# Layer 1's 3x3 convolutions by 4x4 output tiles and two images per pass, in place of 4x2 tiles and one image

## The chip, the cores and the metric

One core of a Trainium2 chip runs the whole program in one launch. The metric is the device time of one execution in microseconds; lower is better. In this text PE is TensorE (matmul), PEld its weight load, DVE is VectorE, ACT is ScalarE, POOL is GpSimd and SP is SyncE, which here only issues DMAs.

## The reference

The input x has 4 images of 512 channels, 32x32, in float32. Layer 0 is a Mamba block over the 1024 pixels of each image as tokens, layer 1 a position-attention block. Both are added to their input, and both take the input through a group norm. Layer 1 is what the change rewrites:

```python
x_top = conv1x1(x, w_top); x_center = conv1x1(x, w_center)     # 64 channels each
x_bottom = conv3x3(x, w_bottom)                                # 512 -> 512
sp = softmax over all pairs of pixels (x_center^T x_top)       # 1024 x 1024 per image
sp = sp @ x_bottom^T ; reshape to (512, 32, 32)
return conv3x3(x + sp, w_out)                                  # 512 -> 512
```

So each image needs two 3x3 convolutions with 512 channels in and out, called b (w_bottom) and o (w_out) below, with the attention between them.

## The kernel before

**Layer 0** is ordered by a planner of the kernel's own (`Plan`). Every step names its engine, an estimate of its time, what it reads and writes, and a due time (`prio`); a greedy pass over all steps writes each engine's queue in the order in which it would start them. The selective scan is cut into 32 blocks (4 images x 4 groups of 256 channels x 2 halves of 512 tokens) of 16 states each, one state of one block being one unit of due time, so that layer 0 runs from 0 to 512 in due times. Per unit, ACT makes the decay (L837) and the scaled input (L849), PE transposes (L875), DVE scans (L889), POOL or DVE multiplies by C (L911, L905) or POOL by B (L864), and PE adds up (L918). The projections of the next image and the output of the one before are spread between.

Also in layer 0, as filler steps (`fill=True`) with due times of their own, lie the weight pieces: the convolutions are Winograd convolutions, and their transformed weights are made on the chip. `transform(u, src, k, prio)` makes piece k of 16 for one convolution: 128 input channels by 128 output channels. POOL does all its additions (three over 768 elements, L1185 to L1195, and nine over 256, L1203 to L1205), ACT two scalings (L1177, L1178), and SP stores the result to the DRAM tensors `u_b` and `u_o` (L1212). The pieces use scratch cut from a tile called `work`, which later becomes the first image's tile. They come at

```python
for k in range(2 * NPC):                       # NPC = 16 pieces per convolution
    transform(u, src, k % NPC, -5 if k < PRM['t0'] else PRM['tg'] * (k - PRM['t0']))
```

with t0 = 7 and tg = 18.5: seven before the first unit, the others one per 18.5 units. `first_image` loads and normalises image 0 at the end of layer 0.

**Layer 1** has no planner: it is written in program order, and the framework (Tile) lists each engine's queue, earlier instructions first when they can run. For each image b the code is: `scores(b)` (1x1 convolutions, the 1024x1024 product `psc`, exponentials `st`), `conv3("b{b}")`, `attend` (product `pat` of `st` with the convolution's result, added into the image xg), `conv3("o{b}")`, transposition back and output. `norm(b + 1)` is drawn through a generator between the first products of `attend`.

A convolution works on tiles of 4x2 outputs: 8 x 16 = 128 tiles per image, one per PE row. The input transform first combines rows (tiles `e`, `f`, `g`, `h`, `k`, `l`, `rr`), in three pairs (1,2), (3,4), (0,5) of the six row indices p, on ACT, POOL and DVE, then columns into `v` (four column indices q, L1488 to L1491, DVE). For each of the 6 x 4 = 24 pairs (p, q) PE accumulates four chunks of 128 channels into a PSUM bank `m` (five banks), with the weights `uw` loaded from u (L1499, L1503); a bias product (L1508) is added at (1,1). ACT and DVE take m into `n` (L1511, L1519), POOL and DVE combine the rows into `y` (L1524 to L1543). For `o`, PE transposes `y` back (`po`, L1589) and DVE adds it to the layer's input (L1594), which is stored to the output.

Of the kernel before, what the change touches and what calls it, by code (L numbers as in the profile page):

```python
# [8 lines left out]
F32 = mybir.dt.float32  # L9
AF = mybir.ActivationFunctionType  # L10
# [161 lines left out]
def mamba_then_pab_kernel(  # L172
# [54 lines left out]
    for name, src in (("b", b_bottom), ("o", b_out)):  # L227
        t = cpool.tile([1, C], F32, tag=f"brow_{name}", name=f"brow_{name}")
        nc.scalar.dma_start(
            t.rearrange("o (c p) -> o c p", p=P), src.rearrange("p (c o) -> o c p", o=1)  # L230
        )
        nc.scalar.activation(t, t, AF.Copy, scale=-12.0)
        brow.append(t)

    def padded(b, pool, tag):

        xg = pool.tile([P, NCC, HH + 2, WW + 2], F32, tag=tag, name=f"xg_{b}")
        nc.gpsimd.memset(xg[:, :, 0, :], 0.0)
        nc.gpsimd.memset(xg[:, :, HH + 1, :], 0.0)
        nc.gpsimd.memset(xg[:, :, 1 : HH + 1, 0], 0.0)  # L240
        nc.gpsimd.memset(xg[:, :, 1 : HH + 1, WW + 1], 0.0)
        return xg

    NP6, NQ = 6, 4
    ub, uo = (
        [
            dram.tile([NP6, P, NCC, C], F32, tag=f"u_{n}_{q}", name=f"u_{n}_{q}")
            for q in range(NQ)  # L250
        ]
        for n in "bo"
    )
    x1 = [
# [25 lines left out]
    with ExitStack() as l0:  # L280
# [53 lines left out]
        work = cpool.tile([P, NCC * (HH + 2) * (WW + 2)], F32, tag="image", name="work")  # L334
# [6 lines left out]
        def dram_set(name, shape, n=B):  # L341
# [10 lines left out]
            "tg": 1, "tm": 1, "tp": 1, "tn": 1, "to": 2,  # L352
# [38 lines left out]
        for ring, rows in (("tg", 9), ("tm", 6), ("tp", 6), ("tn", 6), ("to", 4), ("to", 4)):  # L391
            cells.setdefault(ring, []).append(work[:, at * QC : (at + rows) * QC])
            at += rows
# [689 lines left out]
        def first_image(prio):  # L1083

            spl = {}
            stat = buf(None, None, "")
            chunks = [buf(None, None, "") for c in range(NCC)]

            def inner(c):
                return image[0][:, c, 1 : HH + 1, 1 : WW + 1]  # L1090

            def make():
                image[0] = padded(0, cpool, "image")

            step("POOL", 1.2, make, [], [pieces, *chunks], prio - PRM["fl"])
            for c in range(NCC):
                for h in range(NH):
                    n = HH // NH
                    step(
                        "SP", 0.4,  # L1100
                        lambda c=c, h=h, n=n: nc.sync.dma_start(
                            inner(c)[:, h * n : (h + 1) * n, :],
                            x1[0][h][c * P : (c + 1) * P, :].rearrange("p (h w) -> p h w", w=WW),
                        ),
                        [x1s[0][h]], [chunks[c]], prio - PRM["fl"], kb=768,
                    )

                def stats(c=c):
                    if c == 0:
                        spl["mv"] = spool.tile([P, NCC, 2], F32, tag="mv", name="mv_image")  # L1110
                    bs = spool.tile([P, NH, 6], F32, tag="bs", name=f"bs_image_{c}")
                    n = HH // NH
                    for h in range(NH):
                        nc.vector.bn_stats(bs[:, h, :], inner(c)[:, h * n : (h + 1) * n, :])
                    nc.vector.bn_aggr(spl["mv"][:, c, :], bs)

                step("DVE", 1.45, stats, [chunks[c]], [stat], prio + 4)
            prio += 4
            pm = buf("mm", [P, T], "pm_image")
# [571 lines left out]
```

## Time and profile before

| | |
|---|---|
| three timed runs | 3069.58, 3080.04, 3082.79 us (median 3080.04) |
| the profiled execution's own time | 3079.09 us |
| its span in the profile | 3077.3 us |
| granted TensorE clock, mean | 0.97 of full |
| busy share of the span: PE, DVE, ACT, POOL | 91%, 74%, 59%, 69% |
| layer 0 / layer 1 | 0 to 2044 us / 2044 to 3077 us |

A group of the profile is one line of the source on one engine with its operation, output and inputs: x its count, busy time in us, the mean of one in ns, then the idle time of the engine ahead of it and who ended that. A float32 matmul shows as two PE records. Where a helper issues the instruction, groups are told apart by the names of the tiles.

### The profile page before, as it was taken

What the parts mean: (1) busy time and instruction counts of PE and PEld (TensorE: products, weight loads), DVE (VectorE), ACT (ScalarE), POOL (GpSimd) and SP (SyncE); (2) the same over time, 40 slices, a digit from 0 to 9 for tenths busy, and PEclk for the clock granted to TensorE, in tenths of its full rate; (3) what the DMA queues carried; (4) which work ended last, traced back from release to release, by engine and by line L of the source; (5) the groups of instructions that cost most, each with busy time, mean ns of one, the idle gap of its engine ahead of it and who ended that gap; (6) DMA issues with size and microseconds to landing.
All of it is one profiled execution on the core that took longest, in us unless ns stands there. A gap on an engine that the chain in (4) does not pass through costs nothing.

```text
span 3077.3 us, 36921 instructions
## 1 busy us (share of the span) xinstructions
PE 2789.0 (91%) x11896; PEld 1669.4 (54%) x11896; DVE 2290.1 (74%) x2989; ACT 1822.0 (59%) x3300; POOL 2125.4 (69%) x1197
## 2 busy tenths in 40 slices
PE   6788789999889999888999968879999999999998
PEld 2556566566666666666666656644444444444444
DVE  4579999888999988989988879985285375346344
ACT  4679878898888888788898879941120030030000
POOL 6989888899978899978889999952151143134222
PEclk9899899999999999999999989999999999999999
DMA  6756455577645577745567654448178458628827
GB/s 183 219 171 210 142 158 155 174 233 241 210 139 173 179 222 239 237 128 162 164 189 222 213 159 140 134 121 319 43 266 316 155 175 317 245 85 312 302 86 260
DMA packets 404537, 600.07 MB, mean 195 GB/s; under 512 B 47192, under 2 KB 246104, under 8 KB 379768
## 3 DMA queue, kind: packets, MB, share of 16 engines
q1 hardware_dynamic: 395536, 583.18, 59.8%
q10 hardware_dynamic: 8648, 14.26, 1.3%
q8 instruction: 95, 1.56, 0.2%
q14 instruction: 98, 0.80, 0.1%
q0 software_dynamic: 160, 0.26, 0.0%
HBM read 500.60 MB, written 96.99 MB: 194 GB/s over the span
## 4 chain that ended last, share of the span: by engine, by line
PE 40%; DVE 12%; ACT 6%; DMA 4%; POOL 4%; issue 3%; SPq 0%; DVEq 0%; POOLq 0%; ACTq 0%
PE m_o L1503 10%; PE m_b L1503 8%; PE pat L1553 7%; DVE da L889 5%; PE y L918 3%; PE po L402 2%; PE psc L1380 2%; PE u L875 2%; DMA uw_b<-u_b 2%; POOL da L911 2%; DVE dbx L889 2%; DVE u L889 1%; PE pz L402 1%; PE pp L728 1%; ACT sc L849 1%
## 5 line engine op out<-in xcount | busy, mean ns | idle before, releaser
L911 POOL TENSOR_TENSOR da<-da,cbc 128x1024 f32<-128x1024 f32 x328 | 773.2, 2368 | 114.7 <-DVE da L889 53.1
L849 ACT ACTIVATE sc<-dtxt,bt_sb 128x256 f32<-128x256 f32 x1312 | 578.1, 499 | 99.3 <-PE u L875 98.5
L837 ACT ACTIVATE da<-dt,a_sb 128x512 f32<-128x512 f32 x656 | 454.1, 716 | 78.8 <-PE y L918 62.8
L864 POOL TENSOR_TENSOR dbx<-dtx,bbc 128x1024 f32<-128x1024 f32 x184 | 434.4, 2373 | 10.6 <-DVE carry_sb L894 4.6
L889 DVE TENSOR_TENSOR_SCAN da<-da,carry_sb,u 128x512 f32<-128x512 f32 x328 | 403.1, 1262 | 42.4 <-PE u L875 40.1
L918 PE MATMUL y<-ident,da 128*128 128x128 f32 x2624 | 366.6, 284 | 72.1 <-POOL da L911 69.9
L889 DVE TENSOR_TENSOR_SCAN da<-da,u 128x512 f32<-128x512 f32 x328 | 397.9, 1213 | 31.0 <-PE u L875 29.0
L875 PE MATMUL u<-ident,sc 128*128 128x128 f32 x2624 | 389.2, 282 | 23.5 <-DVE da L889 14.8
L918 PEld LDWEIGHTS y<-ident,da 128*128 128x128 f32 x2624 | 309.4, 146 | 180.6 <-POOL da L911 132.3
L875 PEld LDWEIGHTS u<-ident,sc 128*128 128x128 f32 x2624 | 314.2, 145 | 113.5 <-issue 34.2
L1503 PE MATMUL m_b<-uw_b,v_b 128*128 128x512 f32 x768 | 337.6, 596 | 17.5 <-issue 8.3
L1503 PE MATMUL m_o<-uw_o,v_o 128*128 128x512 f32 x768 | 334.1, 595 | 4.5 <-DVE v_o L1422 4.1
L402 PE MATMUL pxm<-xt,winc 128*128 128x341 f32 (+4 forms) x768 | 251.0, 470 | 21.7 <-DVE xs L661 10.5
L1503 PEld LDWEIGHTS m_b<-uw_b,v_b 128*128 128x128 f32 x768 | 143.4, 190 | 204.1 <-issue 187.1
L402 PE MATMUL pz<-xt,winc 128*128 128x512 f32 x512 | 244.8, 599 | 8.8 <-DMA winc<-in_w_in_dram 2.5
L837 ACT ACTIVATE u<-dt,a_sb 128x512 f32<-128x512 f32 x368 | 245.5, 681 | 11.9 <-DVE da L889 6.7
L1503 PEld LDWEIGHTS m_o<-uw_o,v_o 128*128 128x128 f32 x768 | 145.6, 191 | 190.2 <-issue 181.7
L918 PE MATMUL y<-ident,dbx 128*128 128x128 f32 x1472 | 215.4, 285 | 36.0 <-DVE dbx L905 24.7
L918 PEld LDWEIGHTS y<-ident,dbx 128*128 128x128 f32 x1472 | 175.7, 147 | 88.2 <-DVE dbx L905 25.8
L1553 PE MATMUL pat<-y_b,st 128*128 128x512 f32 x512 | 221.7, 593 | 0.1
L661 DVE SCALAR_TENSOR_TENSOR xs<-pxm,cw_sb,xs 128x341 f32<-128x341 f32 (+8 forms) x288 | 163.6, 569 | 60.6 <-ACT xs L652 53.6
L1511 ACT ACTIVATE e_b<-m_b 128x512 f32<-128x512 f32 x24 | 14.3, 596 | 316.4 <-PE m_b L1503 300.0
(220 smaller groups left out, 4315.4 us busy)
## 6 DMA issues: line engine op xcount, KB each, us to landing
cbc<-bcd SPq DMA_DIRECT2D x512, 256.0 KB, 3.6
uw_b<-u_b SPq DMA_DIRECT2D x96, 1024.0 KB, 5.1
uw_o<-u_o SPq DMA_DIRECT2D x96, 1024.0 KB, 4.9
bbc<-bcd SPq DMA_DIRECT2D x184, 256.0 KB, 3.9
u_b<-work SPq DMA_DIRECT2D x192, 128.0 KB, 3.0
u_o<-work SPq DMA_DIRECT2D x192, 128.0 KB, 3.4
winc<-in_w_in_dram SPq DMA_DIRECT2D x72, 256.0 KB, 3.7
szd<-sz SPq DMA_DIRECT2D x32, 512.0 KB, 4.0
```

The costliest lines, as they stand in the source:

```text
L402: lambda k=k, lhs=lhs, rhs=rhs: nc.tensor.matmul(p()[:, at : at + cols], lhs(), rhs(), start=(k == 0), stop=(k == n - 1)),
L661: nc.vector.scalar_tensor_tensor(u()[:, first:end], p()[:, first - k - at + before : n - k + before], cw[k], u()[:, first:end], ALU.mult, ...
L837: nc.scalar.activation(t, dt()[:, j], AF.Exp, scale=a_sb[:, at : at + 1])
L849: nc.scalar.activation(sc()[:, k], dtxt()[:, k], AF.Copy, scale=bt[:, at, s : s + 1])
L864: lambda: nc.gpsimd.tensor_mul(hc(), dtx(), b_bc().to_broadcast([P, 2, T])),
L875: nc.tensor.transpose(u()[:, k * P : (k + 1) * P], sc()[:, k, j, :], ident)
L889: nc.vector.tensor_tensor_scan(ht, *((hc()[:, j], u()) if on_act else (u(), hc()[:, j])), carry_sb[:, j, s : s + 1] if h else 0.0, ALU.mul ...
L911: lambda: nc.gpsimd.tensor_mul(hc(), hc(), c_bc().to_broadcast([P, 2, T])),
L918: nc.tensor.matmul(y[j]()[:, k, :], hc()[:, j, k * P : (k + 1) * P], ident, start=(s == 0 and k == 0), stop=(s == NS - 1 and k == NK - 1), ...
L1380: nc.tensor.matmul(pt, top[:, m * P : (m + 1) * P], center[:, h * T : (h + 1) * T], start=True, stop=True,)
L1503: nc.tensor.matmul(m[q], v[:, q, k, c, :], w[:, c, :], start=(c == 0), stop=(c == NCC - 1 and not extra),)
L1553: nc.tensor.matmul(pt, st[m][:, 2 * P * j + h : 2 * P * (j + 1) : 2], xb[m // 2][:, m % 2, :], start=(m == 0), stop=(m == NMC - 1),)
```

## The change

Layer 1 takes tiles of 4x4 outputs: 36 products per tile in place of 24, with 8 x 8 = 64 tiles per image, so that two images fill the 128 rows of one pass. The images lie in SBUF sorted by the remainder of row and column mod 4 (`grid`, pitch 9), with zeros where a border is needed. The loop goes over pairs of images. Rows and columns both use the six-point transform (`rows`, `cols`); intermediates `e`, `h`, `m0` of the columns lie in PSUM. The attention goes image by image; `by_image` sorts the first convolution's result by image with ACT copies. Behind the first image's attention the first row pair of the second convolution is made for that image, and for the second image chunk by chunk.

The weight pieces grow with it: in layer 0 a piece has two column steps per row group where it had one (POOL), two more scalings on ACT per row group, and 18 stores where it had 12. Only 16 + EARLY = 22 pieces are made there, at the due times that pieces 0 to 21 had. The other ten, all of w_out, are made by `piece` on DVE, written behind the attentions of the first pair of images. `first_images` also takes the statistics of image 1; `norm` of images 2 and 3 comes at the head of the second pair's turn.

```diff
-    NP6, NQ = 6, 4
+    NP = 6
+    PITCH = 9
+    SIDE = 4 * PITCH
+    FIRST = (26, 0, 9, 18, 27, 1)
+    def grid(xg, c):
+        return xg[:, c].rearrange("p (b y) (k x) -> p b y k x", y=PITCH, x=PITCH)
...
+    def normalise(xg, c, t, scale, bias):
+        v = t.rearrange("p (y b x k) -> p b y x k", y=8, b=4, x=8)
+        for b in range(4):
+            nc.scalar.activation(
+                grid(xg, c)[:, b, 0:8, :, 0:8].rearrange("p y k x -> p y x k"), v[:, b],
+                AF.Identity, bias=bias[:, c : c + 1], scale=scale[:, c : c + 1],
+            )
...
-                step(name, 2.28, columns, [b], [o], prio, fill=True)
-                for q in range(NQ):
...
+                step("ACT", 0.9, more, [b], [sc], prio, fill=True)
+                for q in (1, 3, 0):
+                    if q:
...
+                        step(name, 2.28, columns, [b, sc] if q == 3 else [b], [o], prio, fill=True)
+                    for k, qq in enumerate((q, q + 1) if q else (0, 5)):
...
-        for k in range(2 * NPC):
+        for k in range(NPC + EARLY):
...
+        def wide(name):
+            return lp.tile([P, L], F32, tag="a", name=name, bufs=16)
...
+        def rows(pair, r, m, cs=slice(0, NCC)):
+            xg = image[m]
+            x = [xg[:, cs, a : a + TI, :].rearrange("p c i x -> p c (i x)") for a in FIRST]
+            r0, r1 = (t[m][:, cs].rearrange("p c i x -> p c (i x)") for t in r)
+            if pair == (1, 2):
+                stt(r0, x[2], -4.0, x[4], ALU.mult, ALU.add)
+                stt(r1, x[1], -4.0, x[3], ALU.mult, ALU.add)
+                (nc.vector if cs.stop - cs.start == 1 else nc.gpsimd).tensor_sub(r1, r0, r1)
+                stt(r0, r0, 2.0, r1, ALU.mult, ALU.subtract)
+            elif pair == (3, 4):
+                nc.gpsimd.tensor_sub(r1, x[4], x[2])
+                nc.gpsimd.tensor_sub(r0, x[3], x[1])
+                stt(r1, r0, -2.0, r1, ALU.mult, ALU.add)
+                stt(r0, r0, 4.0, r1, ALU.mult, ALU.add)
+            else:
+                stt(r0, x[2], -5.0, x[4], ALU.mult, ALU.add)
+                stt(r0, x[0], 4.0, r0, ALU.mult, ALU.add)
+                stt(r1, x[3], -5.0, x[5], ALU.mult, ALU.add)
+                stt(r1, x[1], 4.0, r1, ALU.mult, ALU.add)
...
+        def cols(name, r, v, m=slice(0, 2), cs=slice(0, NCC)):
...
+            e, h, m0 = (bank(f"{t}_{name}")[:, :n] for t in ("e", "h", "m0"))
...
+            eng = nc.gpsimd if n == 2 * NCC * HT else nc.vector
+            stt(shaped(e), x[2], -4.0, x[4], ALU.mult, ALU.add)
+            stt(shaped(f), x[1], -4.0, x[3], ALU.mult, ALU.add)
+            tt.tensor_sub(w[2], laid(e), laid(f))
+            tt.tensor_add(w[1], laid(e), laid(f))
+            eng.tensor_sub(shaped(g), x[4], x[2])
+            tt.tensor_sub(shaped(h), x[3], x[1])
+            stt(w[4], laid(h), -2.0, laid(g), ALU.mult, ALU.add)
+            stt(w[3], laid(h), 2.0, laid(g), ALU.mult, ALU.add)
+            tt.tensor_sub(shaped(m0), x[2], x[0])
+            stt(w[0], laid(m0), -4.0, laid(g), ALU.mult, ALU.add)
+            eng.tensor_sub(shaped(m3), x[5], x[3])
+            stt(w[5], laid(h), -4.0, laid(m3), ALU.mult, ALU.add)
...
+                    for q in (2, 1, 4, 3, 0, 5):
...
+                        if q in (2, 4):
+                            nc.scalar.activation(e, m[q], AF.Copy, scale=w[q])
+                        elif q == 1 and not edge:
+                            stt(n[0][:, 0], m[1], w[1], e, ALU.mult, ALU.add)
+                            stt(n[0][:, 1], m[1], w[1], e, ALU.mult, ALU.subtract)
+                        elif q == 1:
...
+                        elif q == 3:
+                            stt(m[4], m[3], w[3], e, ALU.mult, ALU.subtract)
+                            stt(m[3], m[3], w[3], e, ALU.mult, ALU.add)
+                            src = n if edge else (n[0], n[0])
+                            stt(n[1][:, 0], m[3], 4.0, src[1][:, 0], ALU.mult, ALU.add)
+                            stt(n[1][:, 1], m[4], 8.0, src[1][:, 1], ALU.mult, ALU.add)
+                            tt.tensor_add(n[0][:, 0], m[3], n[0][:, 0])
+                            stt(n[0][:, 1], m[4], 2.0, n[0][:, 1], ALU.mult, ALU.add)
+                        else:
+                            t = n[q // 5][:, q // 5]
+                            stt(t, m[q], w[q], t, ALU.mult, ALU.add)
...
+        def piece(k):
...
+            for x in range(3):
+                t = lp.tile([P, 2 * NCC, QC], F32, tag="u", name=f"g_{k}_{x}", bufs=5)
+                nc.sync.dma_start(t[:, 0:6:5], taps[:, x, 0:3:2])
+                nc.sync.dma_start(t[:, 6], taps[:, x, 1])
+                tt.tensor_add(t[:, 1], t[:, 0], t[:, 5])
...
+            for q, far, near in ((1, 1.0, 1.0), (3, 4.0, 2.0)):
...
+                stt(f[0], g[2], far, g[0], ALU.mult, ALU.add)
+                stt(f[1], g[1], -near, f[0], ALU.mult, ALU.add)
+                stt(f[0], g[1], near, f[0], ALU.mult, ALU.add)
...
+        for b in range(0, B, 2):
+            if b:
+                norm(b)
+            norm(b + 1)
+            sa = scores(b)
+            conv3(f"b{b}", ub, brow[0], after=by_image(b, xb))
+            sb = scores(b + 1)
+            attend(b, *sa, xb)
+            r = row_tiles(name, (1, 2), True)
+            v = {p: v_tiles(f"{name}_{p}") for p in (1, 2)}
+            rows((1, 2), r, 0)
+            for k, p in enumerate((1, 2)):
+                cols(f"{name}_{p}_a", r[k], v[p], slice(0, 1))
...
+            attend(b + 1, *sb, xb, chunk)
+            if b == 0:
+                for k in range(EARLY, NCC * C // QC):
+                    piece(k)
+            conv3(name, uo, brow[1], v, back(b, b + 2 == B))
```

In the sums of rows (`conv3`, not shown) POOL makes the sums and differences of a row pair's `n` tiles (eight of 1024 elements in the pairs (1,2) and (3,4) together, and two more into y[0]), and DVE six scaled sums of 1024. `back` loads both images' layer input into eight tiles of the ring "a" ahead of the convolution, and stores them after the last row.

## The prediction

> **What bounds the kernel now.** I read the busy shares in 40 slices first (one digit per 76.9 us, tenths of a slice), then the busy time by stage.
>
> ```profile
> PE   6788789999889999888999968879999999999998
> DVE  4579999888999988989988879985285375346344
> ACT  4679878898888888788898879941120030030000
> POOL 6989888899978899978889999952151143134222
> ```
> ```profile
> 0.00:215.00 215.00, 167.75 (x620) 96.59 (x621) 115.99 (x198) 129.10 (x220) 173.37 (x149) 0.96 0.68 188
> 215.00:1122.00 907.00, 813.87 (x4397) 562.28 (x4396) 824.99 (x1117) 781.13 (x1416) 816.17 (x456) 0.97 0.62 185
> 1122.00:1837.00 715.00, 634.41 (x3444) 440.80 (x3444) 618.76 (x824) 603.61 (x1103) 656.55 (x363) 0.95 0.63 194
> 1837.00:2044.00 207.00, 174.19 (x1037) 125.04 (x1036) 199.13 (x265) 171.58 (x320) 179.61 (x84) 0.97 0.49 134
> 2044.00:3077.30 1033.30, 998.81 (x2405) 444.67 (x2404) 531.20 (x588) 136.63 (x244) 299.70 (x148) 0.99 0.61 218
> ```
> Columns: stretch, its length, then busy time of PE, PEld, DVE, ACT, POOL. Two regimes. Layer 0 (to 2044) has four engines at 84 to 92%, so whoever gets more work there becomes late. Layer 1 is PE alone: 998.8 of 1033.3, DVE 51%, POOL 29%. The pieces of transformed weights (their tile is called work) lie in layer 0:
>
> ```profile
> L1203 POOL TENSOR_TENSOR work<-work x96: 712/731/767, 25.4 to 1822.0; 128x256 f32<-128x256 f32 x96
> ...
> L1185 POOL TENSOR_TENSOR work<-work x32: 1802/1820/1854, 23.6 to 1809.6; 128x768 f32<-128x768 f32 x32
> ```
> Next the groups of layer 1, with mean ns after the busy time:
>
> ```profile
> L1503 PE MATMUL m_b<-uw_b,v_b 128*128 128x512 f32 x768 | 337.6, 596 | 17.5 <-issue 8.3 <-DMA uw_b<-u_b 8.3 <-DVE y_b L1543 0.9
> ...
> L1519 DVE SCALAR_TENSOR_TENSOR n_b<-m_b,n_b 128x512 f32<-128x512 f32 x48 | 32.8, 684 | 77.9 <-PE m_b L1503 77.9
> ...
> L1489 DVE TENSOR_TENSOR v_b<-rr_b 128x1024 f32<-128x1024 f32 x12 | 32.0, 2670 | 0.0
> ...
> L1488 DVE TENSOR_TENSOR v_b<-rr_b 128x1024 f32<-128x1024 f32 x12 | 14.6, 1216 | 0.0
> ...
> L1541 DVE SCALAR_TENSOR_TENSOR y_o<-y_o,y_o 128x1024 f32<-128x1024 f32 x4 | 13.4, 3352 | 11.5 <-POOL y_o L1533 11.5
> ...
> L1542 DVE SCALAR_TENSOR_TENSOR y_o<-y_o,y_o 128x1024 f32<-128x1024 f32 x4 | 4.8, 1212 | 0.0
> ```
> PE barely waits, DVE waits for PE. The same DVE shape takes 1.21 us or 2.7 to 3.4 when its two inputs are in SBUF and POOL works beside it. Last, how layer 1's queues are ordered:
>
> ```profile
> 2067.51 1.20 DVE L1385 TENSOR_REDUCE mx<-st 128x1 f32<-128x1024 f32 x1
> 2068.64 1.27 DVE L1462 SCALAR_TENSOR_TENSOR rr_b<-h_b,g_b 128x1088 f32<-128x1088 f32 x1
> 2069.84 1.21 DVE L1385 TENSOR_REDUCE mx<-st 128x1 f32<-128x1024 f32 x1
> ```
> Work written later (rr) stands between reductions written earlier: the framework fills gaps, so the ten pieces, written behind both attentions, can be drawn beside them.
>
> **PE in layer 1: -172.** Old: 8 passes (four images, two convolutions) of 24 products over 4 channel chunks, 768 accumulations in 337.6 + 334.1 = 671.7 us, 0.875 each (a record is half of one). New: 4 passes of 36, 576 accumulations, 504: -168. Bias matmuls (L1508, 9.0 us for 8) halve: -4.5. Scores, attention and transposes stay in number.
>
> **DVE beside the passes: +32.** PE needs 126 us per pass. DVE per pass: evictions 4x10 + 2x14 = 68 at 0.684 (L1519) = 46.5; columns 6x10 at about 0.68 = 41; rows 18 of 1152 elements at 1.28x1152/1088 (L1462) = 24; sums 6 at 1.21 = 7. That is 119; starts follow 0.07 us closer than durations (the three rows above), 152 times: 109, or 87%. The order is tighter than that sounds: columns of the next row must be ready when PE ends the present one, and edge rows (0 and 5) cost 14 evictions instead of 10. The second convolution trades rows and columns made early (22) for 32 transposed adds at 0.414 (13). To this comes SBUF contention. In layer 1 now, 186 instructions with two SBUF inputs take 100 us more than at their shortest, 0.54 each; a new pass has 48 (rows 18, columns 24, sums 6): +26, so DVE 135 against 126. Five product banks of 3.5 us each are 17 us of slack, which smooths single late spots but not a pass that is long as a whole; I take +8 per pass, four times, with bounds 0 and +27. The upper one: POOL's work in a pass is 12 columns at 1.27 (L1524) = 15, six rows at 2.53 (L1458) = 15 and ten sums at 2.35 (L1540) = 24, so its share rises from 29% to 54/126 = 43%; 0.54 becomes 0.80, or +39, and edge rows that wait for POOL's sums add a few: 148 to 153.
> The Trainium skill, "SBUF — State Buffer", section "Who interferes with whom", says that such a DVE instruction and a POOL instruction that reads SBUF exclude each other for the whole instruction. In kind the trace agrees (3.35 beside 1.21 for L1541 and L1542). By it each of the 48 could wait a whole POOL instruction, an estimate of 48x2.35 = 113 us per pass, and then the change loses outright; L1462, two SBUF inputs and 1.29 on average, shows that many miss POOL.
>
> **Ten pieces on DVE: +20.** A piece is 18 instructions of 128 elements (between 0.15 for 1 and 0.41 for 256: 0.28) and 6 of 768 (between 0.68 and 1.21: 0.95): 10.7, with close starts 9.0; ten 90 to 107. The window is scores (21) and two attentions (2x55.5), 132 us of PE. DVE's own work there is 66: 8 maxima (10), rows and columns of the first image (14), of the second by chunk (28), 32 adds (9), evictions (5). 156 to 173 exceed 132 by 24 to 41; some loads start under the last products. Stores move 23.6 MB, 108 us at layer 1's 218 GB/s, also in the window. The loads and stores add 12 issues of about 0.46 per piece to SP's queue, 55 us in all, ahead of the second convolution's weight loads. Behind the last piece stand its store (3.4, the median of u_o's) and the first weight load (4.9); in PE's queue the first product of that convolution waits for both, because each product sums over all chunks, and everything after it stands behind. I take +20; 0 to +95.
>
> **Other seams: +35.** Image 3's and 2's normalisation now waits at the end of the first pair for slots of one 16-deep ring (8 output tiles, 6 v tiles): load 8.0 (x1t), statistics 5.5, 16 ACT parts at 0.46 (L1371) 7.4; today it hides under attention. Behind it in PE's queue stand the scores of image 2 and, through the rows of both images, the next pass. +20; 0 if the slots come early, +40 if the two images follow one after the other. Last chunk to first product 5 twice; 4 MB instead of 2 stored at the end: +5. Frames, regrouping (32 ACT copies of 0.59, ACT 13% busy) and 12.8 us of POOL adds per image: nothing, covered by 55 us of attention; uncovered 5 to 10 us a pair.
>
> **Layer 0: +55.** Old piece on POOL: 3x1.82 + 9x0.73 = 12.0. New: 3x1.82 + 18x0.73 = 18.6, +6.6; on ACT six more of 0.42 (L1414), +2.5; six more stores on SP, 0.46 each. 22 pieces instead of 32, at unchanged times: eight by the start, fourteen more until block 16 (1122 us), none after. Start: +52 on POOL, 41.6 idle of which 20 lies before its first piece: +32. To 1122: 816 + 92 = 908 us of POOL; the highest share shown is 0.96 (DVE, 199 of 207), 908/0.96 = 946: +39. From 1122 to 1837 POOL loses 119, but PE holds 89% and DVE 87%: -20 (0 to -40). At the seam to layer 1, image 0 is normalised by 16 ACT parts of 0.46 where four DVE instructions of 0.81 do it now, behind the same root, +4; image 1's eight loads (again by ACT's queue in layer 1) and statistics (8x0.67 on DVE) have inputs since batch 1 and fit in the 8 us in which PE waits for its first v now: nothing, or +6 without that gap. Bounds +25 (net POOL time alone) and +95.
>
> **Sum**, on the profiled 3079.1 (1 us under the median): 3079.1 - 172 + 32 + 20 + 35 + 55 = 3049; I say 3048. A measurement can tell about 0.5%, 15 us.
>
> **Rivals.** *Slower, DVE becomes the bound of the passes:* at 153 us a pass each adds 27, 108 for 32: 3124. It decides from 142 us a pass, where the four extra 16 eat the net gain; for it the contention rows, against it DVE's idle time today and the banks. *The pieces are not beside attention* but after it: 107 + 8 for 20: 3143; for it their place in the text, against it the reordering shown. *Better, the extra work is absorbed:* layer 0 +25, passes free, seams 15, pieces 20: 2967; for it PE's 97% in layer 1 today, against it layer 0's four full engines.
>
> **How the numbers follow.** Forecast 0.47 (own range 3005 to 3095: faster 0.33, same 0.10, slower 0.04), DVE-bound 0.27, late pieces 0.11, absorbed 0.15. DVE-bound leaves 0.02 faster or same; so faster 0.49, same 0.12, slower 0.39. The range runs from 2960 to 3140: about a tenth lies on each side.
>
> **What would show it.** PE 576 accumulations; layer 0's end near 2100 with POOL nearly full to 1170 and under 80% after; DVE over 85% in the passes, its SBUF pairs lengthened; a PE gap of some 20 us on u_o before the first m_o; another of 20 before the third image's scores. Wrong: layer 0 at 2050 or 2140, passes at 150, or a gap of 90.

## The result and the profile after: slower by 4.5%

The changed kernel takes 3214.8 us (median; 3213.6 to 3215.9), the kernel before 3078.8 in the same session: ratio 1.0446, 95% interval 1.0422 to 1.0470. The forecast was 3048 and its range ended at 3140. All readings below are of a profiled execution of 3215.0 us with a span of 3212.7.

First the busy shares in 40 slices, one digit per 80.3 us.

```profile
PE   7867578999878999988999988859877876987887
DVE  4627789978899989999989889958787866851485
ACT  4757778898787898887899899932320004151100
POOL 7899889999999999876679899923230421311140
```

Before, PE stood at 9 in layer 1 from the 28th slice to the last but one; of these slices two are at 9 now, one is at 6 and the others are at 7 and 8. At the start PE falls to 5 while POOL is at 8 and 9. The same by stage (stretch, length, then busy time of PE, PEld, DVE, ACT, POOL, the granted clock, DMA share, GB/s):

```profile
0.00:243.00 243.00, 178.71 (x621) 103.93 (x622) 110.83 (x191) 142.27 (x266) 205.25 (x206) 0.89 0.66 185
243.00:1216.00 973.00, 826.33 (x4395) 565.63 (x4394) 831.95 (x1124) 809.36 (x1498) 916.08 (x588) 0.94 0.62 185
1216.00:1908.00 692.00, 628.63 (x3469) 437.42 (x3467) 624.87 (x834) 598.25 (x1092) 553.13 (x254) 0.97 0.55 172
1908.00:2133.00 225.00, 176.89 (x1016) 123.80 (x1016) 199.18 (x271) 179.38 (x334) 174.96 (x85) 0.91 0.41 130
2133.00:3212.70 1079.70, 875.74 (x2008) 390.21 (x2008) 718.25 (x1287) 227.41 (x356) 275.74 (x186) 0.90 0.57 189
```

The stretches end at the same events as those of before (215, 1122, 1837, 2044, the end): some 10 us behind the first scan of blocks 1, 16 and 28, and at layer 1's first product. So layer 0 ends 89 us later and layer 1 is 46 us longer, though PE works 123 us less in it. PE's idle time in layer 1 went from 34.5 us to 204.0. What PE waited for there (engine, what it wanted to do, whom it waited for, us in total, times, longest):

```profile
PE pz L1622 <- DVE v_o L1505: 37.7, 2, 21.6
PE m_o L1546 <- DVE v_o L1504: 31.6, 11, 4.7
PE po L1694 <- DVE n_o L1594: 30.3, 4, 9.0
PE m_b L1546 <- DVE a_b L1562: 20.8, 2, 10.4
PE psc L1411 <- issue: 17.7, 1, 17.7
PE psc L1411 <- ACT center L1398: 12.4, 1, 12.4
...
PE m_o L1546 <- DMA uw_o<-u_o: 4.2, 5, 1.7
```

Three kinds are to be told apart. At `pz` the second image's attention cannot start, twice, because the columns of the first image hold all three banks of the ring that attention uses. At `m_b` (a_b) and `po` (n_o) the edge rows and the transposes wait for the chain that adds and subtracts row pairs. At `psc` the scores wait for ACT, also where the view says "issue": in the first pair ACT is at that time normalising the second image and then taking center and top out of their banks (2153.5 to 2158.3), and psc starts at 2157.9:

```profile
2143.58 9.90 ACT L255 ACTIVATE image<-x1t,gnb_im,grstd_im 128x256 f32<-128x256 f32 x16 [23.52 <-DMA x1t<-x]
```

The pieces' wait on u_o is nearly nothing. The chain, in the groups (busy time, mean ns of one):

```profile
L1546 PE MATMUL m_o<-uw_o,v_o 128*128 128x512 f32 x576 | 271.6, 629 | 46.3 <-DVE v_o L1504 31.6 <-DVE n_o L1572 10.3 <-DMA uw_o<-u_o 4.2
L1546 PE MATMUL m_b<-uw_b,v_b 128*128 128x512 f32 x576 | 253.9, 602 | 23.4 <-DVE a_b L1562 20.8 <-ACT st L1415 1.7 <-DVE n_b L1572 1.0
...
L1585 POOL TENSOR_TENSOR n_b<-n_b,n_b 128x1024 f32<-128x1024 f32 x8 | 23.6, 2949 | 0.6
...
L1584 POOL TENSOR_TENSOR a_b<-n_b,n_b 128x1024 f32<-128x1024 f32 x8 | 21.7, 2710 | 24.8 <-DVE n_b L1575 24.8
...
L1594 DVE SCALAR_TENSOR_TENSOR n_b<-n_b,n_b 128x1024 f32<-128x1024 f32 x4 | 13.4, 3355 | 8.6 <-POOL n_b L1585 8.6
```

Of the ten sums of a pass on POOL, six stand between the last middle row and the first edge row; in the first convolution they run one behind the other from 2264.2 to 2281.2. In the second, from the first of these six to the transposes that wait for them (start, length, then the instruction):

```profile
2585.17 2.34 POOL L1584 TENSOR_TENSOR a_o<-n_o,n_o 128x1024 f32<-128x1024 f32 x1 [19.17 <-DVE n_o L1575]
...
2589.96 3.35 DVE L1594 SCALAR_TENSOR_TENSOR n_o<-n_o,n_o 128x1024 f32<-128x1024 f32 x1 [4.94 <-POOL n_o L1585]
...
2593.45 1.51 PE L1694 MATMUL po<-ident,n_o 128*128 128x128 f32 x6 [6.14 <-DVE n_o L1594]
```

A product record has a mean of 629 ns on m_o and 602 on m_b (596 on m_b before): after a gap PE is also slower for a while, as e8_fill shows below.

### The profile page after: what moved, and what is told of

Read it like the earlier page. It is cut to its first block, busy times and chain, and to the rows that moved or that the text cites. A ratio compares the mean times of both kernels' runs of the same rounds, so it can differ in the third digit from the quotient of the medians.

```text
span 3212.7 us, 37724 instructions
## 1 busy us (share of the span) xinstructions
PE 2686.3 (84%) x11504; PEld 1621.0 (50%) x11504; DVE 2485.1 (77%) x3703; ACT 1956.7 (61%) x3541; POOL 2125.2 (66%) x1317
## 5 line engine op out<-in xcount | busy, mean ns | idle before, releaser
L1546 PE MATMUL m_o<-uw_o,v_o 128*128 128x512 f32 x576 | 271.6, 629 | 46.3 <-DVE v_o L1504 31.6
L415 PE MATMUL pxm<-xt,winc 128*128 128x345 f32 (+4 forms) x768 | 252.3, 469 | 28.8 <-DVE xs L674 10.2
L1546 PE MATMUL m_b<-uw_b,v_b 128*128 128x512 f32 x576 | 253.9, 602 | 23.4 <-DVE a_b L1562 20.8
L1628 PE MATMUL pat<-xb,st 128*128 128x512 f32 x512 | 231.0, 612 | 10.5 <-DVE h_o L1507 8.2
L1546 PEld LDWEIGHTS m_o<-uw_o,v_o 128*128 128x128 f32 x576 | 113.3, 201 | 199.7 <-issue 132.4
L415 PEld LDWEIGHTS pxm<-xt,winc 128*128 128x128 f32 x768 | 141.4, 196 | 106.1 <-issue 35.9
L1546 PEld LDWEIGHTS m_b<-uw_b,v_b 128*128 128x128 f32 x576 | 110.5, 193 | 166.7 <-issue 135.1
```

The costliest lines, as they stand in the source:

```text
L415: lambda k=k, lhs=lhs, rhs=rhs: nc.tensor.matmul(p()[:, at : at + cols], lhs(), rhs(), start=(k == 0), stop=(k == n - 1)),
L1546: nc.tensor.matmul(m[q], v[q][:, c].rearrange("p m t -> p (m t)"), uw[:, i, :], start=(c == 0), stop=(c == NCC - 1 and not extra),)
L1628: nc.tensor.matmul(pt, st[m][:, 2 * P * j + h : 2 * P * (j + 1) : 2], xb[m][:, b % 2, :], start=(m == order[0]), stop=(m == order[-1]),)
```

## The experiments

Theory: the saving on PE is there, and it is lost to hand-overs between PE and the engines that feed it (the bank ring of attention, POOL's sums, the order of the transposes) and, in layer 0, to POOL's extra work. Rival: VectorE's amount of work bounds layer 1, as the forecast's slower case has it. Differences below are differences of ratios to the kernel before, times 3079; a ratio's interval is about 0.0025 to each side of it at the changed kernel and half to one times that elsewhere, so a difference is good to 8 to 10 us.

| run | edit to the changed kernel | median us | ratio, 95% interval | against the changed kernel |
|---|---|---|---|---|
| e1_banks | other banks for attention's columns | 3175.6 | 1.0327 [1.0311, 1.0342] | -37 |
| e2_spread | layer 0's pieces spread out | 3188.0 | 1.0362 [1.0344, 1.0379] | -26 |
| e3_noq3 | columns 3, 4 of those pieces left out | 3125.0 | 1.0159 [1.0143, 1.0176] | -88 |
| e17_scale_stays | the same, ACT's scalings stay | 3129.5 | 1.0157 [1.0139, 1.0175] | -89 |
| e4_nopieces | no pieces on DVE | 3201.4 | 1.0413 [1.0391, 1.0436] | -10 |
| e10_banks_nopieces | e1 and e4 | 3146.0 | 1.0214 [1.0199, 1.0229] | -71 |
| e5_sums | row sums on DVE | 3155.3 | 1.0244 [1.0227, 1.0261] | -62 |
| e6_late | transposes behind row 0's products | 3174.8 | 1.0308 [1.0293, 1.0324] | -42 |
| e7_order | image normalised after the evictions | 3227.7 | 1.0480 [1.0459, 1.0500] | +10 |
| e8_fill | idle matmuls in the gap | 3209.2 (one run) | | |
| e11_four | e1, e2, e5, e6 | 3072.9 | 0.9983 [0.9972, 0.9994] | -143 |
| e12_early0 | e11, 16 pieces on DVE | 3080.0 | 1.0009 [0.9996, 1.0023] | -135 |
| e13_early3 | e11, 13 pieces on DVE | 3107.0 | 1.0097 [1.0078, 1.0116] | -107 |
| e14_evict | e11, evictions on DVE | 3079.6 | 1.0003 [0.9993, 1.0014] | -136 |
| e15_half | e11, half of the wide piece work on POOL | 3101.7 | 1.0067 [1.0048, 1.0087] | -117 |
| e16_both | e14, e15, later statistics | 3107.0 | 1.0087 [1.0070, 1.0103] | -111 |

**The bank ring of attention.** In `cols`:

```diff
-            e, h, m0 = (bank(f"{t}_{name}")[:, :n] for t in ("e", "h", "m0"))
+            whole = n == 2 * NCC * HT          # the columns beside attention are narrower
+            e, h, m0 = (
+                (bank(f"{t}_{name}") if whole else pm.tile([P, T], F32, tag="m", name=f"{t}_{name}"))[:, :n]
+                for t in ("e", "h", "m0")
+            )
```

> Against the changed kernel (3215 us). The columns that are made during attention take their three scratch tiles from the five product banks instead of the three banks that attention uses. Theory (banks): PE's two waits at the start of the second image's attention (21.6 and 16.1 us on v_o) go, and with them part of the slow matmuls behind them: 3165 to 3185 us, the second attention 20 us shorter in each pair. Rival (DVE's work itself is late, whatever bank it is written to): the attention keeps its length or the wait moves to the first m_o; 3205 to 3215 us.

3175.6, as expected. PE's waits in layer 1 of e1_banks:

```profile
PE m_o L1550 <- DMA uw_o<-u_o: 43.8, 6, 21.0
PE po L1698 <- DVE n_o L1598: 30.3, 4, 9.0
PE m_b L1550 <- DVE a_b L1566: 20.7, 2, 10.4
```

`pz` is gone from the list, both attentions run in one piece of 109 us, and the waits of m_o on v_o at the first column step (L1504, here L1508) fall from 31.6 to 11.4 us. But waits of 43.8 us on u_o, the stores of the pieces, stand in the first pair where 4.2 stood, 21.0 and 20.8 of them in two gaps. The bank wait had covered them.

**The pieces.** For e4_nopieces, and on top of e1_banks for e10_banks_nopieces:

```diff
-            if b == 0:
-                for k in range(EARLY, NCC * C // QC):
-                    piece(k)
-            conv3(name, uo, brow[1], v, back(b, b + 2 == B))
+            conv3(name, ub, brow[1], v, back(b, b + 2 == B))
```

> The ten pieces on VectorE are left out, and the second convolutions read the weights of the first (so w_out's own transformed weights are left out of the result). Theory from the trace of the changed kernel (the pieces lie beside conv tail and attention; first m_o waits 1.7 us for u_o): 5 to 12 us less, 3203 to 3210 us. The prediction's +20 would give 3195 us, its rival of pieces behind the attention 3110 to 3125 us.

> The attention's columns in product banks (as in e1_banks, 3176 us) and no pieces on VectorE (as in e4_nopieces, so w_out's own transformed weights are left out). Theory: the bank wait and the pieces cover each other. With the bank wait gone the pieces' stores set the first m_o (43.8 us on u_o in e1_banks), so leaving them out is worth the difference between e1_banks' two pairs, 28 to 40 us: 3135 to 3150 us, and no wait on u_o over 2 us. Rival (the pieces' price is 13 us, as measured with the bank wait in place, and the wait on u_o only takes the place of other late work): 3160 us or more.

With the bank wait in place the pieces cost 10 us, at the edge of what can be told, without it 1.0327 - 1.0214, or 35 us. e10_banks_nopieces lies within its theory, e4_nopieces 2 us below its own: the two costs cover each other, and neither run alone tells the price of the pieces.

**The sums of row pairs.** In `conv3`, three operations:

```diff
-                nc.gpsimd.tensor_add(s, ns[0][t], ns[1][t])
-                nc.gpsimd.tensor_sub(d[t], ns[0][t], d[t])
+                tt.tensor_add(s, ns[0][t], ns[1][t])
+                tt.tensor_sub(d[t], ns[0][t], d[t])
...
-                    nc.gpsimd.tensor_add(y[0][t], y[0][t], y[2][t])
+                    tt.tensor_add(y[0][t], y[0][t], y[2][t])
```

> The ten sums and differences of row pairs of each pass (128x1024 each) go from POOL to VectorE: 40 instructions of about 1.2 us more on VectorE in layer 1. Theory (PE waits on the chain of these sums before the edge rows: 20.8 us on a_b, 30.3 and 10.3 on n_o, and the two engines lengthen each other's instructions): the wait on a_b halves, those on n_o fall by a third, 3175 to 3200 us. Rival (VectorE's quantity of work bounds the passes, as the prediction's slower case has it): passes longer by up to 12 us each, 3220 to 3260 us.

3155.3, more than the theory asked, and the opposite of what the rival needs: VectorE got 40 instructions more and each pass got shorter. The two first convolutions of e5_sums by stage, and its waits:

```profile
2187.00:2312.00 125.00, 124.93 (x292) 54.99 (x291) 108.30 (x171) 36.73 (x62) 24.09 (x12) 1.00 0.85 282
...
2703.00:2828.00 125.00, 124.67 (x292) 54.82 (x291) 101.28 (x140) 36.35 (x62) 24.11 (x12) 1.00 0.86 286
```
```profile
PE po L1694 <- DVE n_o L1594: 17.3, 4, 4.4
```

125 us a pass with PE full and a granted clock of 1.00: the forecast's 126, which the changed kernel missed by 13 (139). VectorE's own time in the first of these passes fell from 111.6 to 108.3 though it has ten instructions more. L1584 takes 1.2 us on VectorE where POOL took 2.7, and L1594 takes 1.2 where it took 3.35: the sums on POOL were slow themselves, stood in series, and made their neighbour slow; this run takes all three away and doesn't tell their shares. The wait on a_b is gone from the list.

**The order of the transposes.** In `conv3`:

```diff
                     if edge and after:
-                        after(3 * k, y)
+                        for z in ((1, 2, 0), (3,))[k]:
+                            after(z, y)
...
-                if after:
-                    after(1, y)
-                    after(2, y)
```

> In the second convolutions the transposes of rows 1 and 2 (and in the first their regrouping) come behind the products of row 0 instead of ahead of them. Theory (the transposes stand in PE's queue and wait for the sums while the products behind them are free): most of the 30.3 us on n_o goes, half comes back as waits of row 0's products for banks: 3190 to 3203 us. Rival (the sums are late for whatever stands there): the wait moves whole to m_o, 3210 to 3218 us.

3174.8: twice what was expected. The wait of po on n_o leaves the list altogether. What comes back, in e6_late:

```profile
PE m_o L1546 <- DVE n_o L1572: 10.9, 3, 6.0
PE m_o L1546 <- DVE a_o L1562: 9.4, 2, 4.7
```

Only the second line is new, 9.4 us for 30.3. The second convolutions shorten from 175 and 165 us to 154 and 145; the first ones stay at 139, since their regrouping is not on PE.

**Layer 0.** First the due times, then columns 3 and 4 (in e3_noq3 `more`, ACT's scalings, goes as well):

```diff
-PRM = dict(..., t0=7, tg=18.5, ...)
+PRM = dict(..., t0=2, tg=23, ...)
```
```diff
-                    if q:
+                    if q == 1:                 # q == 3 stores the tile of q == 1
                         o = buf("to", [P, 2, 2, QC], f"to_{tag}_{rows.start}_{q}")
```

> Only the due times of the 22 pieces of layer 0 change: 2 instead of 7 at the start, then one every 23 units instead of every 18.5, so that they end near unit 437 of 512 instead of 259. Theory (POOL is full to block 16 and has room after): layer 0 ends 40 to 70 us earlier than at 2133, total 3145 to 3175 us. Rival (the sum of the work on POOL, ACT and SP is what counts, or the stores): the end of layer 0 within 15 us of 2133, total 3200 us or more.

> In layer 0's 22 pieces the columns 3 and 4 are not computed: nine POOL operations and six ACT scalings less per piece, and the tile of columns 1 and 2 is stored in their place, so all stores stay (the weights of columns 3 and 4 are left out). Theory (POOL's work is what layer 0 pays for): POOL loses 22 x 6.6 = 145 us, nearly all of it before unit 259, and layer 0 ends at 2030 to 2060 instead of 2133; total 3115 to 3145 us. Rival (the six added stores per piece on SP's queue, and the seam): layer 0 still ends after 2110, total 3190 us or more.

> The changed kernel without the nine POOL operations of columns 3 and 4 in each of the 22 pieces of layer 0, but, unlike e3_noq3, with ACT's six scalings (the weights of columns 3 and 4 are left out). Theory (POOL's work is what layer 0 pays for): as e3_noq3, 3118 to 3140 us. Rival (ACT's 43 us of scalings share it): 3140 to 3175 us, and 3190 us if they carry it.

From the start to some 9 us behind the last scan, in turn: before, the changed kernel, e2_spread, e3_noq3, e17_scale_stays.

```profile
0.00:2038.80 2038.80, 1785.03 (x9480) 1222.39 (x9481) 1754.82 (x2396) 1685.42 (x3056) 1825.71 (x1049) 0.96 0.61 184
```
```profile
0.00:2118.60 2118.60, 1798.63 (x9472) 1225.22 (x9472) 1761.34 (x2409) 1727.80 (x3183) 1849.42 (x1131) 0.95 0.58 176
```
```profile
0.00:2095.60 2095.60, 1805.18 (x9472) 1230.24 (x9472) 1759.55 (x2409) 1727.97 (x3182) 1847.62 (x1131) 0.95 0.60 177
```
```profile
0.00:2024.30 2024.30, 1770.90 (x9472) 1213.44 (x9472) 1759.22 (x2409) 1682.82 (x3052) 1709.41 (x933) 0.96 0.62 184
```
```profile
0.00:2038.10 2038.10, 1779.87 (x9472) 1213.21 (x9472) 1758.76 (x2409) 1722.95 (x3183) 1709.77 (x933) 0.96 0.62 182
```

POOL is the last busy time of a line, ACT the one before it. The last scan itself ends at 2029.7, 2109.1, 2086.4, 2014.9 and 2029.0. Taking 140 us from POOL brings it 80 us earlier (e17_scale_stays). With ACT's 40 us of scalings taken as well (e3_noq3) it comes another 14 earlier, but the profiled execution was the fastest of four in e3_noq3 and the slowest of four in e17_scale_stays (3120.1 and 3134.9), and the ratios of the two are the same: a price of the scalings isn't shown. The 132 stores (six a piece) of columns 3 and 4 are in both. Up to the first scan of block 16, e3_noq3 has the work of the kernel before on POOL (979 and 980 us) and these stores on top, and reaches it at 1113 where 1112 stood, so the stores alone cost nothing that shows; in the changed kernel POOL waits 13.0 us for them up to there (L1232).

Spreading the same POOL work, e2_spread, brings 23 us and not the 40 to 70 of its theory: the first scan of block 4 comes at 367 instead of 448, of block 16 at 1131 instead of 1206, of block 28 at 1875 instead of 1897. Crowding was somewhat over a quarter of the loss. The rest was there however the work was placed, although POOL has only 22 us more than before in all. Of the 57 us that e2_spread's layer 0 is still longer than before, the last block holds 13 (61 us for 48; the two images' statistics stand among its scans); the other 44 build up between blocks 9 and 28, and what makes them is open. POOL's total alone doesn't tell it: e17_scale_stays has 116 us less on POOL than the kernel before, and its last scan comes no earlier.

**The first scores.** `norm(b + 1, True)` does all but the 16 ACT parts and returns these; `scores` calls them behind its evictions of center and top:

```diff
-            norm(b + 1)
-            sa = scores(b)
+            sa = scores(b, norm(b + 1, True))
```

> The normalisation of a pair's second image on ACT comes behind the evictions of the first image's center and top instead of ahead of them. Theory: PE's waits for center (17.7 and 12.4 us ahead of the first psc) fall by about 10 us each, and the rows of the second image are still there when the scores end: 3195 to 3205 us. Rival (the second image's rows become late instead): the same time appears ahead of the first m_b, 3212 us or more.

3227.7, a miss for the theory. PE's waits of 17.7 and 12.4 ahead of psc fell to about 8 and 8, and the first convolutions took 151 and 143 us instead of 139: VectorE's rows wait for the second image, which now comes later from ACT.

**The clock after a gap.**

> The changed kernel with 24 matmuls into an unused product bank ahead of the second image's attention, where PE waits 21.6 and 16.1 us. They compute nothing that is used. Theory (TensorE comes out of a gap with a lower clock): with the gap mostly filled the first 32 matmuls of that attention take 13.9 us instead of 16.4, and the granted clock there rises. Rival (these matmuls are slow because of what runs beside them): they stay near 16.4. Total 3205 to 3220 us either way.

```diff
+            if chunk:
+                pf = pm.tile([P, T], F32, tag="m", name=f"pf_{b}")
+                for k in range(24):
+                    nc.tensor.matmul(pf, xb[k % 8][:, 0, 0:P], xb[k % 8][:, 1, :],
+                                     start=(k == 0), stop=(k == 23))
             pz = bank(f"pz_{b}")
```

In the second pair the filling reached to the end of the wait. The same 17 us there, in the changed kernel and with the filling (the granted clock is the third number from the end):

```profile
2946.00:2963.00 17.00, 9.88 (x20) 4.71 (x21) 8.21 (x25) 0.12 (x1) 0.00 (x0) 0.66 0.00 0
```
```profile
2946.00:2963.00 17.00, 17.00 (x43) 7.80 (x42) 7.45 (x23) 0.22 (x1) 0.00 (x0) 1.00 0.00 0
```

Behind the gap the first four attention matmuls take 1.19, 1.06, 1.06 and 1.06 us, the fifth 0.76, and from there 0.59; behind the filling the first takes 0.68 and the second already 0.59. The first 32 span 14.0 us for 15.9. So a gap of 16 us costs PE another 2 us. In the first pair a wait of 10.3 us came behind the filling, and the slow start was there as before. The Trainium skill, "TensorE: Matmul & The Clock Gate", Part 1 (the HAM clock gate), says that the array falls to half its clock after an idle window of about 3.4 us and needs as much sustained work to come back; the 1.06 for 0.59 (from start to start 0.86 for 0.43) and the 4 us until it is full again agree with that; the length of gap from which it happens no run here shows. In this one run, then, PE's slow start came with the gap and went with it.

**The four edits together.**

> The edits of e1_banks, e2_spread, e5_sums and e6_late together. Theory (each took away its own wait): 39, 27 and 60 us are taken off 3215, and of e6_late's 40 about 20, since e5_sums leaves only 17 of the 30 us on n_o: 3069 us, 3050 to 3085. Rival (the waits stand behind one another, so that one that goes lets the next come out): 3110 us or more.

3072.9, as the theory added it up: ratio 0.9983 with an interval of 0.9972 to 0.9994, a gain too small to matter. In e11_four, layer 0 and layer 1:

```profile
0.00:2105.00 2105.00, 1809.88 (x9498) 1230.81 (x9499) 1765.41 (x2417) 1729.51 (x3185) 1847.54 (x1131) 0.95 0.60 177
2105.00:3065.90 960.90, 844.98 (x2007) 376.30 (x2005) 711.51 (x1326) 227.63 (x356) 174.86 (x146) 0.94 0.64 213
```

Layer 1 is 72 us shorter than before (961 for 1033) where the forecast had 85, and layer 0 is 61 us longer (2105 for 2044) where it had 55. The forecast's sum fits this kernel better than the changed one: most hand-overs come in time here (PE still waits 43.2 us for u_o, and 30 for ACT ahead of psc), and the gain in layer 1 is used up in layer 0.

**Trying for more.** All of these are edits to e11_four. The first two:

```diff
-    EARLY = 6
+    EARLY = 0          # e13_early3: 3, with t0=2, tg=28
-PRM = dict(..., t0=2, tg=23, ...)
+PRM = dict(..., t0=3, tg=33, ...)
```

> As e11_four, but all sixteen pieces of the second convolution's weights are made on VectorE in layer 1 and only the first convolution's sixteen in layer 0 (3 at the start, then one every 33 units). Theory: POOL loses 112 us in layer 0, which ends 40 to 60 us earlier; in layer 1 the six more pieces come out as a longer wait on u_o, 6 x 9 us of VectorE less what is covered, 25 to 55 us: total within 25 us of e11_four. Rival (late pieces are hidden at the 1 to 4 us each that ten of them cost): 25 to 50 us below e11_four.

> Between the two: three of the second convolution's pieces in layer 0, thirteen on VectorE (2 at the start, then one every 28 units). Theory: layer 0 ends 20 to 30 us earlier than in e11_four, u_o is waited for 10 to 25 us longer; total within 15 us of e11_four. Rival as for e12_early0: 12 to 25 us below.

PE's waits for the pieces, in turn e11_four, e13_early3 and e12_early0 (10, 13 and 16 pieces on VectorE):

```profile
PE m_o L1550 <- DMA uw_o<-u_o: 43.2, 5, 21.1
PE m_o L1550 <- DVE o L1674: 72.8, 1, 72.8
PE m_o L1550 <- DMA uw_o<-u_o: 107.8, 4, 104.5
```

With the 4.7 us that e13_early3 has on u_o besides, that is 43.2, 77.5 and 107.8 us: 11 and 10 us for each further piece, about the 10.7 of VectorE that the forecast had counted for one. From ten pieces on nothing more is covered. In return layer 0's last scan ends at 2081, 2079 and 2025. Six pieces less are worth 56 us there, but three are worth 2, which is why e13_early3 is the worst of the three and misses its theory (34 us above e11_four where 15 were allowed); its schedule had also other due times, so the number of pieces isn't the only difference. e12_early0's total lies within its theory, though its wait grew by 65 us and not by 25 to 55.

Evictions on VectorE for the first image (`b % 2 == 0`), in `scores`:

```diff
+                        if b % 2:
+                            nc.scalar.activation(to, part[at], AF.Identity, bias=pb_sb[at])
+                        else:
+                            nc.vector.tensor_scalar_add(to, part[at], pb_sb[at])
```

> e11_four (3073 us) with the first image's center and top taken out of the product banks by VectorE (eight additions of a bias) instead of ACT. Theory (PE's 17.8 and 12.8 us ahead of the first psc are ACT's 9.9 us of normalising the second image, which stands ahead of these evictions): both waits fall to about 5 us, 3050 to 3062 us. Rival (as in e7_order, the time comes back as a wait of the first m_b, because ACT has the same work before the pass can start): 3068 us or more.

The theory's waits fell (about 31 us to about 11 ahead of psc) and the total did not: the rival. The first passes of e14_evict take 133 and 137 us instead of 126 and 125, and in the first of them this line stands:

```profile
DVE r_b L1453 <- ACT image L255: 8.4, 1, 8.4
```

VectorE waits for the normalised image that the evictions were waiting behind. So it seems that ACT's work itself is on the path and not only its order, and that e7_order and e14_evict moved the same wait about; where the second pass's 12 us come from wasn't followed up.

In `piece`, for q = 1, where both factors are 1:

```diff
+                if q == 1:
+                    nc.gpsimd.tensor_add(f[0], g[0], g[2])
+                    nc.gpsimd.tensor_sub(f[1], f[0], g[1])
+                    nc.gpsimd.tensor_add(f[0], f[0], g[1])
+                else:
...
```

> e11_four with three of the six wide operations of each of the ten pieces (128x768 each) on POOL, which is busy for a fifth of that stretch, instead of VectorE. Theory (VectorE is full from the scores to the first m_o, 215 of 245 us, and what is left of the pieces stands behind the attention): VectorE loses 30 us, the 21 us on u_o fall under 6, total 3048 to 3060 us. Rival (the two engines lengthen each other's instructions, as L1594 and POOL's sums did): the wide operations left on VectorE take 1.5 us or more instead of 1.0, total 3068 us or more.

A miss, and the rival's sign didn't show where it was looked for: the wide operations left on VectorE still take 1.0 us (median 0.95). But the pieces' 180 narrow ones (L1657 to L1662) take 76.2 us together instead of 59.6 in e11_four, L1657 0.61 each for 0.31, so over half of the 30 us came back there. The wait on u_o grew from 21.1 to 34.8 at its longest, and attention itself waits 13.1 us for VectorE's rz. VectorE is less busy (138 us for 163 from 2282 to 2460) but waits in its queue:

```profile
DVE o L1680 <- DMA u_o<-o: 11.2, 3, 7.0
DVE r_o L1454 <- POOL r_o L1453: 8.0, 1, 8.0
DVE mx L1416 <- ACT st L1415: 7.3, 7, 4.3
```

In e11_four the first of these is 2.0 (L1675) and the second 2.5. The pieces' output ring has three tiles, which now wait for POOL's slower operations and then for the stores; VectorE's queue stands behind them, and POOL's row difference behind the pieces in POOL's queue.

Both edits, and the statistics' due time 8 units later:

```diff
-            chain(1, [loose(r, 1, c) for c, r in enumerate(("dtx", "dtxt") * 2)], prio)
+            chain(1, [loose(r, 1, c) for c, r in enumerate(("dtx", "dtxt") * 2)], prio + 8)
```

> e14_evict and e15_half together, and the statistics of the second image (8 of 0.67 us on VectorE) behind layer 0's last scans instead of among them. Theory: the three add up, 3020 to 3045 us, faster than the kernel before by 1 to 2%. Rival (they uncover one another): 3055 us or more.

3107.0, 1.0087: the two misses together, as the rival has it. No version here beats the kernel before by more than e11_four's 0.2%.

## Why the prediction was wrong, by its steps

Of the 166 us between forecast (3049) and profiled run, 34 lie in layer 0 and the rest in layer 1. Of the two slower outcomes that it had weighed, a bound VectorE (3124) and late pieces (3143), neither is what happened.

**PE in layer 1, -172: right in count.** PE has 576 accumulations, and where nothing waits a pass takes 125 us (e5_sums). They took 525.5 us in the changed kernel where the forecast had 504, PE being slow behind gaps (e8_fill), and with attention and transposes slowed too PE's busy time fell by 123 us there and by 154 in e11_four. The forecast had no term for that.

**DVE beside the passes, +32: the step that failed.** It took VectorE's amount of work for what could make a pass long, and put "a few" for edge rows that wait for POOL's sums. VectorE's amount left room (111.6 and 104.7 us busy in the 139 us of the two first convolutions, whose first row pair is made ahead of them; 108 of 125 after e5_sums, 87%), and the slower rival, VectorE as the bound, is refuted by e5_sums, which gave it more work and took 62 us off. The loss was latency in a chain: six of the ten sums in series on POOL between the last middle row and the first edge row, 17 us in the first convolution, and in the second convolutions transposes that stand in PE's queue and wait for the same chain while free products stand behind them. Together these cost some 80 us where 32 were put down (e11_four's 143 less the 37 and 26 of e1_banks and e2_spread). The text named the sums with their price, 2.35 each (they took 2.3 to 3.6), and priced them as work and contention, with "a few" for the wait; where PE stands in order behind their end was not asked.

**No step for the banks: +37.** The forecast counted five product banks as slack, but it did not walk through the other ring of three, which attention, transposes and columns share, in program order. That ring made the two gaps of 21.6 and 16.1 us, and e1_banks took them away.

**Ten pieces on DVE, +20 (0 to +95): right in kind, sized by an accident.** The wait of some 20 us on u_o ahead of the first m_o that was announced isn't in the changed kernel (1.7 at most), since the bank gap gives the pieces time; with other banks it is there, twice (21.0 and 20.8 us), and the price is 35.

**Other seams, +35.** The third image's normalisation, put at +20, shows a gap of 8 us before its scores. The time lies elsewhere, 30 us ahead of the first psc of both pairs, where ACT normalises 16 parts at 0.80 us (the forecast used 0.46) and then evicts center and top. In the first pair ACT also issues image 1's eight loads only from 2135 to 2143.5, behind the end of layer 0, though the forecast counted on inputs that had long been there and put them at nothing. Three runs (e7_order, e14_evict, e16_both) moved that wait and none removed it.

**Layer 0, +55: 89.** POOL full to block 16 and at 80% after it, as announced. Until block 16 it lost 94 us where 71 stood (32 and 39; for the start, 52 less the 21.6 of usable idle time is 30), and 74 of them already by block 4: block 0 grew by 29 us and the three after it by 47, with POOL at 89 to 97% in these. After block 16, 23 came back for the 20 put down. At the seam, where image 1's statistics were put at nothing, the last block is 13 us longer (61 for 48). e16_both, with these statistics behind the scans, takes 6 of the 11 that e11_four has there (53 for 59), but its layer 1 starts no earlier (2105.5 for 2104.1).

**The rule on the shared port.** The Trainium skill, "SBUF — State Buffer", section "Who interferes with whom", holds here in kind: L1594 takes 3.35 us beside POOL's sums and 1.22 without them (e5_sums). The estimate of the worst case from it, 113 us per pass, was far off. Each VectorE instruction of a first convolution set against the shortest of its line and shape in these two runs, 17 and 16 us go to lengthening in the changed kernel's two passes, 5 and 4 in e5_sums, where the forecast's own price was 26.

## What to carry to other kernels

When work per pass shrinks on the engine that bounds it, sum up the other engines' work, but then walk once through the bounding engine's queue at each change of phase: for every instruction at its head ask which chain must end and which buffer must come free, and price the chain by its length in series, not by its share of busy time. A cost that one run finds small may be covered by another wait; take the two away together before calling it small. What work taken from a full engine gives back has no fixed rate: 80 us of 140 in e17_scale_stays, 56 of 107 in e12_early0, but 2 of 53 in e13_early3.

## What the runs showed of the hardware

A gap on PE costs more than its length: after 16 us of waiting the next four matmuls of 128x512 took about 1.06 to 1.19 us instead of 0.59, which is 2 us for this gap, and PE's busy time in layer 1 fell from 876 us in the changed kernel to 845 in e11_four with the same matmuls. An operation moved from POOL to VectorE can shorten VectorE's own time: ten additions of 1.22 us more, and the busy time of the stage fell from 111.6 to 108.3, while a VectorE instruction with two SBUF inputs (L1594) took 3.35 us beside POOL's sums and 1.22 without. It isn't so for every neighbour: the wide piece operations on VectorE kept a median of 0.95 us beside POOL's in e15_half, and the narrow L1657 went from 0.31 to 0.61.
